# Two filter buffers outside the tables' room, a table in another's place, and the norms' transfer on the stores' queue

## The chip, the core and the metric

The kernel runs on one core of a Trainium2 chip. Its time is the device time of one execution in microseconds. One more execution was recorded by the profiler; the profile and all answers of its trace are of that one.

## What is computed

Four convolution blocks follow one another on an input of 32 images with 96 channels of 56 by 56 points. Each block normalises its input over groups of three channels and adds its result to the input:

```python
x = x + L0(_gn(x))   # 1x1 expand to 576, 3x3 depthwise, squeeze-excite, 1x1 project
x = x + L1(_gn(x))   # wavelet convolution, three Haar levels, 5x5 depthwise on each
x = x + L2(_gn(x))   # 1x1, 3x3 depthwise, 1x1 with weights and activations rounded to 4 bits
x = x + L3(_gn(x))   # 9x9 depthwise; its kernel is worked out from diff_metric

def _gn(v, G=32, eps=1e-5):
    g = v.reshape(B_, G, C_ // G, H_, W_)
    m = jnp.mean(g, axis=(2, 3, 4), keepdims=True)
    s = jnp.var(g, axis=(2, 3, 4), keepdims=True)
    return ((g - m) / jnp.sqrt(s + eps)).reshape(v.shape)
```

## The kernel before

**Layers 0 and 2 run image by image**, with channels on the partitions. Within them the order of PE, DVE and ACT is written out by hand, in the lists `L0_ORDER` and `L2_ORDER`: each entry is a step, a block of channels and a part of it (`e` expand, `f` first tap, `t` one of the other eight taps, `a` and `c` depthwise on PE, `p` project, `d` add, `o` store), and `+` and `-` shift it by an image. SP and POOL are not in these lists. A planner orders them from costs and due times of its own, and it also orders everything that stands outside such a list. The waits are put in by the framework.

**Layers 1 and 3 run channel by channel**, with image rows on the partitions. There a convolution is a product with a banded matrix for each channel, and SP's order is written out too. Layer 1 takes two channels (a pair) per turn and loads three turns ahead; layer 3 loads four channels ahead (`AHEAD`), and the norms of eight channels (`NN`) at once.

**Layer 0's taps.** Three blocks of an image are filtered on DVE. For each, ACT writes the first tap into one of five buffers `h2s` (L327), DVE adds the other eight taps (L332), and ACT ends the block (L338). Image b uses buffers 3b, 3b+1 and 3b+2, modulo five. In the order's list image 0 begins with `f0`, its later steps contain `f1 m+ t11`, and `f2 a0 t17 t21` come near the end. `m`, `q`, `v`, `w`, `b` and `n` are the steps of the next image's normalisation: negative mean (DVE, L282), sum of squares (ACT, L273), group sum (PE, L278), deviation (DVE L286, then a power on POOL, L288), bias (DVE L292), and the normalised image (ACT, L301).

**The tables.** `tables()` is called while layer 0 starts. `diffusion_kernels` works out layer 3's 9x9 kernels, on DVE and then on POOL. `wavelet_filters` spreads layer 1's filters into three padded tables `zt0`, `zt1`, `zt2` (cleared by POOL at L499, filled by DVE at L510), and SP stores them to DRAM (L511). `diffusion_filters` then clears the first half of `zt1` again (L1127), fills it on POOL (L1125, L1134), and SP stores it as `zdiff` (L1135). The tables lie in two pools which are closed before the pool `late` is opened in their room. Of the five tap buffers, one is allocated before the tables and four in `late`, next to `hab`, `wg` and `hc`:

```python
h2s = [cp.tile([128, H, W], F32, tag="h2", name="h2")]
tables()
late = ctx.enter_context(tc.tile_pool(name="l0l", bufs=1))
h2s += [late.tile([128, H, W], F32, tag=f"h2{i}", name=f"h2{i}") for i in range(3)]
h2s.append(late.tile([128, H, W], F32, tag="h23", name="h23"))
```

From the stored tables, SP copies the banded matrices of all channels from DRAM to DRAM during layer 0 (L522, L549), a few after each image.

**The hand-over between the layers.** The last image of layers 0 and 2 is stored by quarters as soon as each is added: four quarters by six groups of channels, 24 transfers (`store_tile`, L156). Then `store_norm` turns the means and variances of all images into one row per channel (factors, offsets, a bias) and sends it to DRAM from ACT's queue (L120). Layer 1 reads it back with `load_norm` (L600), layer 3 with `load_norms` (L1156), each broadcast to 128 partitions; both need it for their first operation on DVE (L671, L1169). In layer 1's list of loads the two channels' inputs X (L555, L558), matrices (L583 to L585, L656, L658) come first and both norms last; before the list stand four constants (L621). In layer 3 the norms come after the loads of four channels.

Of the kernel before, what the change touches and what calls it, by code (L numbers as in the profile page):

```python
# [10 lines left out]
F32 = mybir.dt.float32  # L11
# [4 lines left out]
ALU = mybir.AluOpType  # L16
# [4 lines left out]
B, C, H, W = 32, 96, 56, 56  # L21
# [59 lines left out]
            nc.sync.dma_start(t, w[n])  # L81


def power(nc, pool, out, in_, e, tag):

    ex = pool.tile(list(in_.shape), F32, tag=f"ex{tag}", name=f"ex{tag}")
    nc.gpsimd.memset(ex, e)
    nc.gpsimd.tensor_tensor(out, in_, ex, ALU.pow)


def channel_stats(nc, pool, x, mv, tag):

    st = pool.tile([C, 2 * NP, 6], F32, tag=f"st{tag}", name=f"st{tag}", bufs=2)
# [2 lines left out]
    nc.vector.bn_aggr(mv, st.rearrange("c a b -> c (a b)"))  # L96


def store_norm(nc, S, pool, psum, mv, dram, bias):


    mc, d, dv, ve = (pool.tile([C, B], F32, tag=f"n{n}", name=f"n{n}", bufs=1) for n in ("mc", "d", "dv", "ve"))
    row = pool.tile([C, 2 * B + 1], F32, tag="row", name="row", bufs=1)
    rstd = row[:, 0:B]
    ps = psum.tile([128, 2, 512], F32, tag="mm", name="pn")
    nc.vector.tensor_copy(mc, mv[:, :, 0])
    nc.tensor.matmul(ps[:C, 0, :B], S.grp, mc, start=True, stop=True)
    nc.vector.tensor_tensor(d, mc, ps[:C, 0, :B], ALU.subtract)
    nc.vector.tensor_tensor(dv, d, d, ALU.mult)
    nc.vector.tensor_tensor(dv, dv, mv[:, :, 1], ALU.add)  # L110
    nc.vector.tensor_tensor(d, mc, d, ALU.subtract)
    nc.tensor.matmul(ps[:C, 1, :B], S.grp, dv, start=True, stop=True)
    nc.vector.tensor_scalar(ve, ps[:C, 1, :B], EPS_GN, None, ALU.add)
    nc.gpsimd.tensor_tensor(rstd, ve, S.mhalf[:C, :B], ALU.pow)
    nc.vector.scalar_tensor_tensor(row[:, B : 2 * B], d, -1.0, rstd, ALU.mult, ALU.mult)
    if bias is None:
        nc.vector.memset(row[:, 2 * B :], 0.0)
    else:
        nc.vector.tensor_copy(row[:, 2 * B :], bias)
    nc.scalar.dma_start(dram, row)  # L120


def run_steps(step, image, order):
# [47 lines left out]
def layer0(ctx, tc, S, x, w, y0, norm1, tables, aside):  # L171
# [9 lines left out]
    nc = tc.nc  # L181
# [57 lines left out]
    diag = cp.tile([128, 2, 9, HALF], F32, tag="diag", name="diag")  # L239
    hpad = padded(cp, nc, 4, F32, "hpad")  # L240
    mv_all = cp.tile([C, B, 2], F32, tag="mv0", name="mv0")
    h2s = [cp.tile([128, H, W], F32, tag="h2", name="h2")]


    tables()
# [2 lines left out]
        for t in range(9):  # L248
            nc.vector.tensor_scalar(diag[:, k - AB, t, :], eye2, wdw[:, COL[k], t : t + 1], None, ALU.mult)
    late = ctx.enter_context(tc.tile_pool(name="l0l", bufs=1))  # L250
    h2s += [late.tile([128, H, W], F32, tag=f"h2{i}", name=f"h2{i}") for i in range(3)]
    hab = late.tile([128, NP, 2, NT], F32, tag="hab", name="hab")
    wg = late.tile([128, ND + 1, C], F32, tag="wg", name="wg")
    h2s.append(late.tile([128, H, W], F32, tag="h23", name="h23"))
    hc = late.tile([128, 2, 2, NT], F32, tag="hc", name="hc")

    ims = {}
# [188 lines left out]
    }  # L446
    with tc.manual_schedule(engines=MANUAL):
        run_steps(step, image, L0_ORDER)
    store_norm(nc, S, sm, psum, mv_all, norm1, S.bias1)


NK = 3
# [2 lines left out]
KW = 5  # L455


def wavelet_filters(nc, cp, cp2, w, z1, z2, z3):
# [14 lines left out]
    nc.vector.tensor_scalar(ws, ws, 0.25, None, ALU.mult)  # L473
    for v, z in enumerate((z1, z2, z3)):
# [12 lines left out]
        G = cp.tile([C, 3, 3, 25], F32, tag="G", name="G")  # L487
        for da in (-1, 0, 1):
            for dp in (-1, 0, 1):
                g = G[:, da + 1, dp + 1]  # L490
                nc.vector.tensor_copy(g, F[:, abs(da), abs(dp)])
                if v == 0:
                    gb = g.rearrange("c (e k) -> c e k", k=KW)[:, 1:4, 1:4]
                    nc.vector.tensor_tensor(gb, gb, base[:, 1 + da : 6 + da : 2, 1 - dp : 6 - dp : 2], ALU.add)
        groups = 2 if v < 2 else 1
        ks = NK if v < 2 else KW
        P = 2 * groups
        Z = (cp2 if v else cp).tile([C, 2, P, LEN, P, ks], F32, tag=f"z{v}", name=f"zt{v}")
        nc.gpsimd.memset(Z, 0.0)  # L499
        for ai in range(2):  # L500
            for ao in range(2):
                rows = slice(MIDL + ao - ai - 4, MIDL + ao - ai + 5, 2)
                for pi in range(P):
                    for po in range(P):

                        d = pi // 2 - po // 2
                        valid = [K for K in range(ks) if abs(groups * (K - ks // 2) + d) <= 2]
                        k0 = groups * (valid[0] - ks // 2) + d + 2
                        g = G[:, ao - ai + 1, po % 2 - pi % 2 + 1].rearrange("c (e k) -> c e k", k=KW)
                        nc.vector.tensor_copy(Z[:, ai, pi, rows, po, valid[0] : valid[-1] + 1], g[:, :, k0::groups])  # L510
        nc.sync.dma_start(z, Z.rearrange("c a p e o k -> c a p (e o k)"))  # L511
        if v == 1:
            room = Z[:, 0]
    return room


def toeplitz(nc, dst, z, phases, rows, step, first, row):
# [87 lines left out]
def layer1(ctx, tc, w, y0, norm, t1, t2, t3, y1, behind):  # L605
# [41 lines left out]
    def load(i):  # L647

        st = {"i": i, **sets[i % NF], "X": [], "T": [None] * 2, "nr": [], "raw": [], "raw2": []}
        for c in (2 * i, 2 * i + 1):  # L650
            X = io.tile([128, 2, B, W4], F32, tag="X", name="X", bufs=8)
            load_halves(nc, X, y0[c // GR][c % GR])
            st["X"].append(X)
            st["raw"].append(load_matrices(nc, pool, t1, c))
            raw = pool.tile([PH, NK * PH], F32, tag="raw2", name="raw2", bufs=4)
            nc.sync.dma_start(raw, t2[c])  # L656
            st["raw2"].append(raw)
            nc.sync.dma_start(st["T3"][c % 2 * HH : (c % 2 + 1) * HH, c % 2], t3[c])  # L658
        for c in (2 * i, 2 * i + 1):
            st["nr"].append(load_norm(nc, norms, norm, c))  # L660
        return st

    def normal(st, j, h):
# [219 lines left out]
def layer2(ctx, tc, S, k2, y1, y2, norm3):  # L883
# [203 lines left out]
    }  # L1087
    with tc.manual_schedule(engines=MANUAL):
        run_steps(step, image, L2_ORDER)
    store_norm(nc, S, sm, psum, mv_all, norm3, None)  # L1090


def diffusion_kernels(nc, cp, w):
# [9 lines left out]
        nc.vector.scalar_tensor_tensor(z[:, i, :], yy[:, 1, :], dm[:, 2 * i + 1 : 2 * i + 2], z[:, i, :],  # L1103
                                       ALU.mult, ALU.add)
    nc.vector.tensor_tensor(z, z, z, ALU.mult)
    r2, arg, two, kern, poi = (cp.tile([C, n], F32, tag=t, name=t) for t in ("r2", "arg", "two", "kern", "poi"))
    nc.vector.tensor_tensor(r2, z[:, 0], z[:, 1], ALU.add)
    nc.vector.tensor_scalar(arg, r2, K_EXP2, None, ALU.mult)
    nc.vector.tensor_scalar(r2, r2, TP * TP, None, ALU.add)

    nc.gpsimd.memset(two, 2.0)
    nc.gpsimd.tensor_tensor(kern, two, arg, ALU.pow)
    power(nc, cp, poi, r2, -1.5, "poi")
    nc.gpsimd.tensor_scalar(kern, kern, K_GAUSS, None, ALU.mult)
    nc.gpsimd.tensor_scalar(poi, poi, K_POI, None, ALU.mult)
    nc.gpsimd.tensor_tensor(kern, poi, kern, ALU.add)
    return kern


# [19 lines left out]
def layer3(ctx, tc, w, y2, norm, td, out):  # L1139
# [40 lines left out]
    with tc.manual_schedule(engines=MANUAL_SP):  # L1180
        for c in range(AHEAD):
            load(c)
        load_norms(0)
        for c in range(-2, C):
            if 0 <= c < C - AHEAD:
                load_norms(c + AHEAD)
# [15 lines left out]
def kernel_body(tc, w, x, out):  # L1202
    nc = tc.nc
    with ExitStack() as ctx:
# [22 lines left out]
        t3 = scratch("twav3", [C, HH, KW * HH])  # L1227

        def tables():
            with tc.tile_pool(name="tables", bufs=1) as tp, tc.tile_pool(name="tables2", bufs=1) as tp2:  # L1230
                kernels = diffusion_kernels(nc, tp2, w)
                room = wavelet_filters(nc, tp, tp2, w, z1, z2, z3)
                diffusion_filters(nc, tp2, kernels, zd, room)

        layer0(tc, S, x, w, y0, norm1, tables,
               [lambda c=c: wavelet_matrices(nc, z1, z2, z3, t1, t2, t3, c) for c in range(C)]
# [134 lines left out]
```

## Time and profile before

| | |
|---|---|
| median of 3 runs | 6552.63 us (6536.49 to 6554.98) |
| profiled execution, its own time | 6547.21 us |
| its span | 6545.4 us |
| PE busy | 6046.6 us (92%) |
| DVE busy | 5167.2 us (79%) |
| ACT busy | 3955.6 us (60%) |
| POOL busy | 223.0 us (3%) |
| DMA, mean | 69 GB/s, 452.93 MB |

The span is what the profiler saw of the execution; the time is measured around it. Rows headed PE, DVE and GB/s cut the span into 40 equal slices of 163.6 us, and each digit is the busy share in tenths. In lists of waits a line names the engine and line that waited, the releaser, the sum in us, how many times, and the longest. In timelines a row has the start and the length in us, the engine (SPq is SP issuing a transfer), the line, the operation, output and input with shapes, how many were merged, and in square brackets the idle time before and what ended it. The chain of waits gives start, length and what ran or was waited for.

### The profile page before, as it was taken

The page shows a single profiled execution, that of the slowest core. Times are in us where ns is not written, and L with a number is a line of the kernel's source. Part 1 is how long each engine was busy: PE and PEld are TensorE (multiplying, and loading weights), DVE is VectorE, ACT ScalarE, POOL GpSimd, SP SyncE. Part 2 cuts the span into 40 slices and gives each one's busy share as a digit, 9 for nine tenths or more (in the row PEclk, how much of TensorE's full clock was granted, in tenths as well). Part 3 has the DMA queues.
Part 4 walks back from the last instruction along what each step waited for, and adds up shares of the span by engine and source line. Part 5 has one row for each costly group of instructions (what it writes and reads, how often), then busy time and mean ns, then how long its engine had stood idle before and what let it go on. Part 6 is the DMA issues. An engine that isn't in the chain of part 4 may idle for free.

```text
span 6545.4 us, 115343 instructions
## 1 busy us (share of the span) xinstructions
PE 6046.6 (92%) x49064; PEld 3627.6 (55%) x49064; DVE 5167.2 (79%) x5468; ACT 3955.6 (60%) x5268; POOL 223.0 (3%) x158
## 2 busy tenths in 40 slices
PE   5989989998998998999969999989999999999699
PEld 3444444444444454445435556567777777778344
DVE  8989989898998998989947666657676767676577
ACT  5556556665666656565535555557676767677355
POOL 4000000000000000000000000000000000000000
PEclk8989989999999999999979999989999999999899
DMA  2375475639538459563755766655869585853788
GB/s 80 27 41 51 41 44 40 47 48 37 46 41 42 48 39 44 36 44 43 10 60 144 138 146 145 144 43 39 52 42 52 40 52 39 52 40 30 159 254 248
DMA packets 1631553, 452.93 MB, mean 69 GB/s; under 512 B 1447406, under 2 KB 1625318, under 8 KB 1627582
## 3 DMA queue, kind: packets, MB, share of 16 engines
q1 hardware_dynamic: 1630814, 445.50, 62.6%
q8 instruction: 386, 6.32, 0.6%
q14 instruction: 129, 1.06, 0.1%
q10 hardware_dynamic: 224, 0.05, 0.0%
HBM read 284.44 MB, written 214.08 MB: 76 GB/s over the span
## 4 chain that ended last, share of the span: by engine, by line
PE 71%; ACT 8%; DMA 6%; SPq 6%; DVE 4%; issue 3%; POOL 1%; POOLq 0%; ACTq 0%; DVEq 0%
PE psd L355 14%; PE psd L1022 10%; PE ps L315 9%; PE psj L413 8%; PE pc L1177 6%; PE ps L1003 6%; PE pc L738 5%; SPq L431 5%; DMA y<-xt 3%; PE psj L1059 3%; PE psj L415 2%; PE psj L416 2%; DVE h L332 2%; ACT hi L975 2%; ACT a L993 2%
## 5 line engine op out<-in xcount | busy, mean ns | idle before, releaser
L332 DVE SCALAR_TENSOR_TENSOR h<-hpad,l_wdw,h 128x3136 f32<-128x3136 f32 x768 | 2659.9, 3481 | 64.2 <-ACT h L327 35.9
L355 PE MATMUL psd<-hpad,diag 64*64 64x392 f32 x13824 | 1245.6, 513 | 31.2 <-issue 31.2
L319 ACT ACTIVATE hpad<-ps,o,s 128x784 f32<-128x784 f32 x640 | 685.0, 1081 | 778.3 <-PE ps L315 775.9
L315 PE MATMUL ps<-xn,l_wexp 96*128 96x392 f32 x2560 | 940.8, 520 | 107.2 <-ACT hpad L319 102.4
L1022 PE MATMUL psd<-apad,diag 64*64 64x392 bf16 x20736 | 929.8, 332 | 105.8 <-ACT a L993 51.6
L355 PEld LDWEIGHTS psd<-hpad,diag 64*64 64x64 f32 x13824 | 570.9, 132 | 694.8 <-issue 648.4
L1022 PEld LDWEIGHTS <-diag 64*64 64x64 bf16 x20736 | 692.2, 107 | 339.2 <-issue 159.1
L315 PEld LDWEIGHTS ps<-xn,l_wexp 96*128 96x128 f32 x2560 | 497.9, 199 | 500.9 <-ACT hpad L319 108.6
L567 ACT COPY T<-raw 32x112 f32<-32x112 f32 (+2 forms) x1440 | 462.6, 384 | 316.5 <-DMA raw<-tdiff 231.8
L993 ACT ACTIVATE u<-ps,o,s 128x784 int16<-128x784 f32 x576 | 536.9, 1003 | 161.1 <-PE ps L1003 142.8
L993 ACT ACTIVATE a<-psd,o,s 128x784 int16<-128x784 f32 x448 | 424.2, 999 | 320.9 <-PE psd L1022 320.9
L413 PE MATMUL psj<-h,wg 128*96 128x392 f32 x1536 | 591.5, 520 | 24.9 <-ACT hpad L319 23.4
L1003 PE MATMUL ps<-hi,l_w1q 96*128 96x392 f32 x1280 | 462.7, 362 | 9.3 <-ACT hi L975 9.2
L1177 PE MATMUL pc<-x,T 128*112 128x416 f32 (+1 forms) x1152 | 415.0, 523 | 58.0 <-DMA raw<-tdiff 58.0
L738 PE MATMUL pc<-x,T 128*112 128x416 f32 (+1 forms) x1152 | 451.2, 528 | 0.0
L1003 PE MATMUL ps<-lo,l_w1q 96*128 96x392 f32 x1280 | 438.3, 342 | 0.0
L413 PEld LDWEIGHTS psj<-h,wg 128*96 128x96 f32 x1536 | 249.1, 166 | 285.0 <-issue 257.4
L1177 PEld LDWEIGHTS pc<-x,T 128*112 128x112 f32 x1152 | 204.8, 178 | 267.7 <-issue 250.8
L338 ACT ACTIVATE hab<-psd,o,s 128x392 f32<-128x392 f32 x256 | 170.9, 672 | 291.2 <-PE psd L355 291.2
L338 ACT ACTIVATE h<-h,o,s 128x3136 f32<-128x3136 f32 x96 | 288.0, 3000 | 17.1 <-DVE h L332 17.1
L327 ACT ACTIVATE h<-hpad,l_wdw 128x3136 f32<-128x3136 f32 x96 | 279.1, 2908 | 31.4 <-DMA zdiff<-zt 30.4
L738 PEld LDWEIGHTS pc<-x,T 128*112 128x112 f32 x1152 | 192.7, 180 | 146.1 <-issue 146.1
(201 smaller groups left out, 6790.5 us busy)
## 6 DMA issues: line engine op xcount, KB each, us to landing
X<-y SPq DMA_DIRECT2D x192, 392.0 KB
xt<-in_x_dram SPq DMA_DIRECT2D x32, 1176.0 KB
y<-xt SPq DMA_DIRECT2D x192, 196.0 KB
y<-y SPq DMA_DIRECT2D x96, 392.0 KB
xt<-y SPq DMA_DIRECT2D x96, 392.0 KB
out_dram<-y SPq DMA_DIRECT2D x96, 392.0 KB
y<-xt SPq DMA_DIRECT2D x90, 392.0 KB
twav<-zwav SPq DMA_DIRECT2D x768, 36.8 KB
```

Source lines behind the costliest of these rows:

```text
L315: nc.tensor.matmul(ps[:, j, :NT], wexp[:, k * 128 : k * 128 + 128], im["xn"][:, j, rows, :].rearrange("c h w -> c (h w)"), start=True, sto ...
L319: nc.scalar.activation(window(im["pad"][k], 128, 0, 0, 2 * i * RT, 2 * RT).rearrange("p r (w j) -> p j r w", j=2), ps[:, :, :NT].rearrange ...
L332: nc.vector.scalar_tensor_tensor(h2, window(im["pad"][k], 128, t // 3 - 1, t % 3 - 1, 0, H), wdw[:, k, t : t + 1], h2, ALU.mult, ALU.add,)
L338: nc.scalar.activation(view, ps, AF.Silu, bias=bi[1][:, c : c + 1], scale=sc[1][:, c : c + 1], accum_out=accum)
L355: nc.tensor.matmul(ps[c * HALF : (c + 1) * HALF, j, :NT].rearrange("p (r w) -> p r w", w=W2), diag[p, k - AB, t, :], v[:, :, j:W:2], start ...
L413: nc.tensor.matmul(out.rearrange("c (r w) -> c r w", w=W2), wg[:, k, :], im["h2"][k][:, rows, j::2], start=(k == 0), stop=False)
L567: nc.scalar.copy(to.rearrange("x t (p s) -> x t p s", p=NPH), v[:, k])
L738: nc.tensor.matmul(ps[:PH, to], st["T"][j][:, h, k, :], st["x"][:, j, h, of], start=False, stop=(n == NK - 1))
L993: nc.scalar.activation(out, ps, AF.Identity, bias=o[:, c : c + 1], scale=s[:, c : c + 1])
L1003: nc.tensor.matmul(ps[:, j, :NT], w1[:, k * 128 : k * 128 + 128], im[part][:, r0 : r0 + RT, :].rearrange("c h w -> c (h w)"), start=(part ...
L1022: nc.tensor.matmul(ps[q, j, :NT].rearrange("p (r w) -> p r w", w=W), diag[p, k, t, :], v, start=(t == 0), stop=(t == 8))
L1177: nc.tensor.matmul(ps[:, :, to], st["T"][:, h, k, :], st["x"][:, h, :, of], start=(n == 0), stop=(n == NK - 1))
```

## The change

- Two of the five tap buffers are allocated before the tables; the other three stay in `late`.
- All tables share one pool. The third wavelet table takes the room of the first after that is stored, and is cleared by DVE instead of POOL. The diffusion kernels reuse their own inputs' room in place of five temporary tiles; the helper `power` is dissolved.
- `store_norm` sends its row from SP, pinned behind all that SP was given before it.
- In layer 1, each channel's norms are loaded right behind its X. In layer 3, the first eight channels' norms are loaded right behind channel 0 instead of behind channel 3.

```diff
-    nc.scalar.dma_start(dram, row)
+    tc.keep_in_program_order(nc.sync.dma_start(dram, row))
...
-    h2s = [cp.tile([128, H, W], F32, tag="h2", name="h2")]
+    h2s = [cp.tile([128, H, W], F32, tag=f"h2{i}", name=f"h2{i}") for i in range(2)]
...
-    h2s += [late.tile([128, H, W], F32, tag=f"h2{i}", name=f"h2{i}") for i in range(3)]
+    h2s += [late.tile([128, H, W], F32, tag=f"h2{i}", name=f"h2{i}") for i in (2, 3)]
...
-    h2s.append(late.tile([128, H, W], F32, tag="h23", name="h23"))
+    h2s.append(late.tile([128, H, W], F32, tag="h24", name="h24"))
...
-        Z = (cp2 if v else cp).tile([C, 2, P, LEN, P, ks], F32, tag=f"z{v}", name=f"zt{v}")
-        nc.gpsimd.memset(Z, 0.0)
+        if v < 2:
+            Z = rooms[v] = cp.tile([C, 2, P, LEN, P, ks], F32, tag=f"z{v}", name=f"zt{v}")
+        else:
+            n = 2 * P * LEN * P * ks
+            Z = rooms[0].rearrange("c a p e o k -> c (a p e o k)")[:, :n].rearrange(
+                "c (a p e o k) -> c a p e o k", a=2, p=P, e=LEN, o=P)
+        (nc.gpsimd if v < 2 else nc.vector).memset(Z, 0.0)
...
             load_halves(nc, X, y0[c // GR][c % GR])
             st["X"].append(X)
+            st["nr"].append(load_norm(nc, norms, norm, c))
             st["raw"].append(load_matrices(nc, pool, t1, c))
...
-        for c in (2 * i, 2 * i + 1):
-            st["nr"].append(load_norm(nc, norms, norm, c))
...
-    r2, arg, two, kern, poi = (cp.tile([C, n], F32, tag=t, name=t) for t in ("r2", "arg", "two", "kern", "poi"))
+    r2, arg, kern = z[:, 0], z[:, 1], yy[:, 0]
...
-    nc.gpsimd.memset(two, 2.0)
-    nc.gpsimd.tensor_tensor(kern, two, arg, ALU.pow)
-    power(nc, cp, poi, r2, -1.5, "poi")
+    nc.gpsimd.memset(yy[:, 0], 2.0)
+    nc.gpsimd.memset(yy[:, 1], -1.5)
+    nc.gpsimd.tensor_tensor(kern, yy[:, 0], arg, ALU.pow)
+    nc.gpsimd.tensor_tensor(r2, r2, yy[:, 1], ALU.pow)
...
         for c in range(AHEAD):
             load(c)
-        load_norms(0)
+            load_norms(c)
...
-            with tc.tile_pool(name="tables", bufs=1) as tp, tc.tile_pool(name="tables2", bufs=1) as tp2:
-                kernels = diffusion_kernels(nc, tp2, w)
-                room = wavelet_filters(nc, tp, tp2, w, z1, z2, z3)
-                diffusion_filters(nc, tp2, kernels, zd, room)
+            with tc.tile_pool(name="tables", bufs=1) as tp:
+                kernels = diffusion_kernels(nc, tp, w)
+                room = wavelet_filters(nc, tp, w, z1, z2, z3)
+                diffusion_filters(nc, tp, kernels, zd, room)
```

More of the change, by code (lines that the diff above doesn't have):

```diff
@@ L81, in load @@
             nc.sync.dma_start(t, w[n])
[L84 to L88, printed above, removed]
 def channel_stats(nc, pool, x, mv, tag):
@@ L96, in channel_stats, with store_norm @@
     nc.vector.bn_aggr(mv, st.rearrange("c a b -> c (a b)"))
-def store_norm(nc, S, pool, psum, mv, dram, bias):
+def store_norm(tc, S, pool, psum, mv, dram, bias):
+    nc = tc.nc
     mc, d, dv, ve = (pool.tile([C, B], F32, tag=f"n{n}", name=f"n{n}", bufs=1) for n in ("mc", "d", "dv", "ve"))
@@ L448, in layer0 @@
         run_steps(step, image, L0_ORDER)
-    store_norm(nc, S, sm, psum, mv_all, norm1, S.bias1)
+    store_norm(tc, S, sm, psum, mv_all, norm1, S.bias1)
 NK = 3
@@ L455, with wavelet_filters @@
 KW = 5
-def wavelet_filters(nc, cp, cp2, w, z1, z2, z3):
+def wavelet_filters(nc, cp, w, z1, z2, z3):
     wb = cp.tile([C, 50], F32, tag="wb", name="wb")
@@ L473, in wavelet_filters @@
     nc.vector.tensor_scalar(ws, ws, 0.25, None, ALU.mult)
+    rooms = {}
     for v, z in enumerate((z1, z2, z3)):
@@ L511, in wavelet_filters @@
         nc.sync.dma_start(z, Z.rearrange("c a p e o k -> c a p (e o k)"))
-        if v == 1:
-            room = Z[:, 0]
-    return room
+    return rooms[1][:, 0]
 def toeplitz(nc, dst, z, phases, rows, step, first, row):
@@ L1089, in layer2 @@
         run_steps(step, image, L2_ORDER)
-    store_norm(nc, S, sm, psum, mv_all, norm3, None)
+    store_norm(tc, S, sm, psum, mv_all, norm3, None)
 def diffusion_kernels(nc, cp, w):
@@ L1109, in diffusion_kernels @@
     nc.vector.tensor_scalar(r2, r2, TP * TP, None, ALU.add)
-    nc.gpsimd.memset(two, 2.0)
-    nc.gpsimd.tensor_tensor(kern, two, arg, ALU.pow)
-    power(nc, cp, poi, r2, -1.5, "poi")
+    nc.gpsimd.memset(yy[:, 0], 2.0)
+    nc.gpsimd.memset(yy[:, 1], -1.5)
+    nc.gpsimd.tensor_tensor(kern, yy[:, 0], arg, ALU.pow)
+    nc.gpsimd.tensor_tensor(r2, r2, yy[:, 1], ALU.pow)
     nc.gpsimd.tensor_scalar(kern, kern, K_GAUSS, None, ALU.mult)
-    nc.gpsimd.tensor_scalar(poi, poi, K_POI, None, ALU.mult)
-    nc.gpsimd.tensor_tensor(kern, poi, kern, ALU.add)
+    nc.gpsimd.tensor_scalar(r2, r2, K_POI, None, ALU.mult)
+    nc.gpsimd.tensor_tensor(kern, r2, kern, ALU.add)
     return kern
```

## The prediction

> **What bounds the kernel now.** I read the slices of the page first, then the list of waits, then the timelines of single engines around the three places that the diff touches.
>
> ```profile
> PE   5989989998998998999969999989999999999699
> DVE  8989989898998998989947666657676767676577
> GB/s 80 27 41 51 41 44 40 47 48 37 46 41 42 48 39 44 36 44 43 10 60 144 138 146 145 144 43 39 52 42 52 40 52 39 52 40 30 159 254 248
> ```
>
> PE is at 9 nearly everywhere, and DVE is close behind it in the first 20 slices (layer 0). Speed inside the stages is not for this diff: it changes nothing in the steady loops. What it can move are the three dips of PE: slice 1 (start), slice 20 (layer 0 to 1, where GB/s is 10) and slice 37 (layer 2 to 3).
>
> *Start.* ACT, DVE and POOL timelines:
>
> ```profile
> 79.09 2.91 ACT L327 ACTIVATE h<-hpad,l_wdw 128x3136 f32<-128x3136 f32 x1 [30.35 <-DMA zdiff<-zt]
> ```
> ```profile
> 67.43 0.15 DVE L282 TENSOR_SCALAR nm<-pn 96x1 f32<-96x1 f32 x1
> 82.03 6.88 DVE L332 SCALAR_TENSOR_TENSOR h<-hpad,l_wdw,h 128x3136 f32<-128x3136 f32 x2 [14.45 <-DMA twav<-zwav]
> ```
> ```profile
> 64.11 3.46 POOL L1125 COPY rev<-kern 96x9 f32<-96x9 f32 x1
> 67.88 0.19 POOL L1125 COPY rev<-kern 96x9 f32<-96x9 f32 x1
> 71.91 1.29 POOL L1134 COPY zt<-rev 96x18 f32<-96x18 f32 x8
> ```
>
> The first tap f1 goes into the second filter buffer, which lies in the pool opened where the tables closed; it waits for the last transfer of all tables. DVE then idles 14.45 us, and has no gap after it (busy 19.89 of the 20 us from 100 to 120, 29.79 of the 30 from 120 to 150). So its next start decides. The POOL rows matter later: the same copy takes 3.46 us while DVE runs taps and 0.19 us once DVE is idle.
>
> *Layer 0 to 1.* SP's waits in 3320 to 3380, chain, DVE timeline:
>
> ```profile
> SPq L156 <- DMA norm<-row: 9.3, 1, 9.3
> ```
> ```profile
> 3362.59 1.48 DMA norm<-row
> 3365.07 0.95 SPq L156
> 3366.06 1.03 SPq L156
> 3367.87 7.05 DMA y<-xt
> 3385.78 3.81 DMA nr<-norm
> ```
> ```profile
> 3389.66 0.92 DVE L671 TENSOR_TENSOR x<-X,nr 128x448 f32<-128x448 f32 x1 [8.63 <-DMA nr<-norm]
> ```
>
> A y store waits for the norms' transfer, with which it has nothing to do: the program has eight completion semaphores for transfers and gives them out in turn over both queues; norm<-row was ordered among the 24 last stores, and the 19th store takes the same semaphore. Six stores sit behind it.
>
> *Layer 2 to 3*, the same: the wait is 7.0 us long, and the norms come after four channels' loads.
>
> ```profile
> 6106.45 0.30 SPq L555 DMA_DIRECT2D X<-y  x1
> 6119.30 0.42 SPq L1156 DMA_DIRECT2D nr<-norm  x1
> ```
> ```profile
> 6124.19 0.62 DVE L1169 TENSOR_TENSOR x<-X,nr 128x448 f32<-128x448 f32 x1 [50.48 <-DMA X<-y]
> 6125.77 24.40 PE L1177 MATMUL pc<-x,T 128*112 128x448 f32 x61 [58.03 <-DMA raw<-tdiff]
> ```
>
> The reader should see that PE waits for x, x for nr, and nr for its place in SP's list.
>
> **The change part by part.**
>
> *1. Start.* Two buffers now lie before the tables, so f1 follows its expansions on ACT at 48.7 instead of 79.09, and q+ follows nm (67.43) at once. DVE could go on at 67.6: gain 14.4. Against it:
> - The third table is cleared on DVE (96x2520), which has no gap between 24 and 67. Nearest row: POOL's clear of this tile, 2.20 us. Bounds: 0.2 (a small DVE operation), and 2.8 (the 3.48 us tap scaled from 3136 to 2520 elements). I take 2.2. It also waits until the first table's store (2.3 MB, issued at 33.47) has read it: the DMA share is 0.97 from 35 to 45 and 0.64 from 45 to 50, so some 44 to 46; DVE reaches the third table's copies at 48.6. Free; if the planner places the clear right behind the second table (40.1), it costs up to 5 us, with the taps queued behind it. POOL's lost 2.20 us (13.3 to 15.4) was off the path.
> - The fewer temporaries: two small POOL memsets (0.16 us each) wait for DVE's last reading of the grid, at 24.8; the power starts at 25.78. 0.3 us, hidden.
> - POOL now copies the diffusion table beside running taps. With nm at 69.6, DVE runs t11 and t08 to 76.7 and t12 to t14 to 87.2. POOL passes two copies per tap (57.2 to 64.1: four in two taps). The nine rev copies end at 74.7 instead of 68.1; then the 2.61 us memset. Here a rule bears: the Trainium skill, "SBUF — State Buffer", "Who interferes with whom", says that a two-input DVE operation blocks GpSimd's reads, not its pure writes. No row here shows a memset under taps. By the rule it ends at 77.3, by the copies' rows (3.5 us) at 78.2. I take the rule; the sum differs by less than 1 us. Of 16 copies some five pass by 87.2; then DVE stands, because b+ needs rstd, which POOL holds behind them. The other 11 take 0.16 each: 89.0; rstd 0.57; t15 starts at 89.9 instead of 99.58. Gain **9.7**.
> - f2 still goes to a buffer over the tables: zdiff is issued at 89.1 and lands 5.8 later (73.23 to 79.05 before), 94.9; f2 ends at 97.8, and its tap t21 is due at 100.3. Slack 2.5 us, so nothing.
> Bounds of this part: 1.8 (rival 1) to 14.4.
>
> *2. norm<-row on SP behind the stores.* A rule of the skill speaks against any gain: "DMA: Bandwidth & Descriptors", "Issuing engines are not separate DMA queues": transfers of all issuing engines share the same 16 engines, so another queue saves issue time only. By it, moving 24 KB is worth 0, and costs one SP issue (0.35 us). By the rows, the wait of 9.3 and 7.0 us goes. The rule is about transfer, the row is about a wait at the issuer; I take the row.
> - Layer 0 to 1: six stores go on at 3354.8 instead of 3364.1. The DMA had emptied by 3357 before; now they queue (about 1.5 us each), so I take 8.4 of 9.3. Layer 1's first load then issues at 3366.7 instead of 3375.07. norm<-row is issued at about 3362.6 as before (its row is ready at 3362.56): its landing is beside the stores'.
> - Layer 2 to 3: 7.0 off. But the row's tile belongs to a pool that layer 3 reuses, and its transfer now comes last; alone it took 1.44 us. I take 1.0, so 6.0. First X load at 6100.4.
>
> *3. The norms' place in layer 1's list.* T0 is the first constant load. Before: nr issued at T0+10.3, x at T0+14.6. Now nr(0) follows X(0): T0+3.9. A raw load issued there (3378.94) had landed by 3382.44, 3.5 us; nr takes 3.8. So x starts at T0+7.7. The step's other loads move back 0.45 us each. Channel 1's x needs nr at T0+12.5, DVE is free at 12.8; ACT's matrix copies of channel 1 end at 16.4, xh at 17.3, xl at 18.4: lowest1 at T0+18.4 instead of 24.9 (3399.96). Gain 6.5. For the next pair nr no longer stands behind the raw load that waits for ACT (3.0 us); that keeps pace and is not counted.
>
> *4. In layer 3.* nr(0) follows load(0): T0+3.2 instead of 12.85. Its earlier landing took 4.9 us; x at T0+8.1 instead of 17.7; loads 1 to 3 move back by one issue and 266 KB, about 1.2 us. T(0) was ready at T0+7.4, PE then runs at its 4.3 us per channel (415.0/96), slower than loads (3.2 us issue). Gain 9.6.
>
> Sum: 9.7 + (8.4 + 6.5) + (6.0 + 9.6) = **40.2 us**. On the profiled execution 6547.2 - 40 = 6507; the median of the runs shown is 5.4 above it, so **6512**. Nothing gives it back: each place has only bound work behind it (DVE in layer 0, PE at 18.0 us per pair in layer 1, PE in layer 3). The eight waits for x in layer 0 (118.4 us) hang on stores that move with DVE.
>
> **The rivals.**
> 1. *The start is given back.* If the planner puts rstd before POOL's table copies, DVE never stands at b+, POOL crawls at two copies per tap, zdiff lands near 105, and t21 waits for f2 until 108.2 instead of 110.0. Gain 1.8, time 6520. Against it: before, the copies came first. Chance 0.2.
> 2. *Hidden anyway.* The last stores are limited by the DMA and not by the issue: busy share 9 from 6080 to 6102 speaks for it, the empty 6070 to 6075 against. Then part 2 gives about 3 instead of 14.4, and the loads crowd the norms: parts 3 and 4 give half (8). With the start at 9.7: 6532. Chance 0.1. If the planner still orders norm<-row among the stores, part 2 is 0: the same case.
> 3. *Slower.* SP's list in layer 0 is ordered by the planner, which now sees an earlier start and a later third table. If its 192 filling jobs fall before x fetches, more images wait; the eight that do now lose 118.4/8 = 15 us each. From three more images on (44) the gain of 40 is used up; four cost 59, and the time is 6552.6 - 40 + 59 = 6572. Against it: the lists hang on the image's own stores. Chance 0.04.
> 4. *More.* POOL is not blocked under taps: start 14, time 6507. Chance 0.05.
>
> **How the numbers follow.** Main case 0.61, by itself 6500 to 6524 (part 1 from 5 to 12, the hand-overs each by 3, the runs' scatter by 8). A measurement here tells 0.3% (19.7 us, 6533) from no change. Faster: 0.61 + 0.2 + 0.05 and half of rival 2, rounded 0.91; same 0.06; slower 0.03. Range 6488 to 6533: it reaches over rivals 1, 4 and most of 2.
>
> **What would show it.** ACT L327's wait for zdiff gone at 48.7; POOL's L1134 copies at up to 3.5 us; DVE's idle before t15 2 to 3 us, with rstd as releaser; no "SPq L156 <- DMA norm<-row"; first L621 load about 8 us sooner after the last add; x (L671) 7.7 us after it; in layer 3 x 8 us after the first X load, and PE 10 us earlier against it. Wrong if: DVE stands at t21 (rival 1), the stores' own spacing grows by what the wait was (rival 2), or the list of waits has more than eight L273 waits for x (rival 3).

## The result, and the profile after

The kernel after takes 6498.39 us (median of 4 runs, 6495.52 to 6506.39) against 6546.09 us (median of 4 runs, 6536.49 to 6554.98): the ratio is 0.9929, 95% interval [0.991, 0.9949], 48 us less by the medians. The profiled executions are 46.05 us apart (6547.21 and 6501.16), and it is these that are taken apart here. The forecast of 6512 was 40 us less. So the total came out near; its terms, as the traces show, did not all.

The slices of the page of after, to be laid beside those of before:

```profile
PE   6989989998998998989969999989999999999699
DVE  8989979898998998989957766657777767676587
GB/s 80 29 41 50 41 43 41 46 44 40 47 41 41 43 47 42 39 41 39 17 60 143 141 155 150 143 36 45 48 42 50 44 49 41 51 38 31 166 253 248
```

The three dips are still there, and at 162 us a slice nothing finer can be read. The milestones of the two traces say more. "Last add" is the very last addition of a layer's last image on DVE; a low-band product is PE's first multiplication of a pair of channels in layer 1 (lowest1).

| stretch | before, us | after, us | gained |
|---|---|---|---|
| start to last add of layer 0 | 3349.7 | 3340.4 | 9.3 |
| to layer 1's first load | 25.3 | 21.3 | 4.0 |
| to the first low-band product | 23.8 | 17.2 | 6.6 |
| first to last low-band product (47 steps) | 878.4 | 855.6 | **22.8** |
| to layer 2's first product | 56.3 | 56.6 | -0.3 |
| to the last add of layer 2 | 1727.4 | 1733.5 | -6.1 |
| to layer 3's first load | 45.6 | 45.3 | **0.3** |
| to layer 3's first product | 19.3 | 9.2 | 10.2 |
| to the end | 419.7 | 420.3 | -0.7 |

*Start.* ACT's and DVE's timelines of after (start, duration, engine, line, what; in brackets the idle time before it and what ended that):

```profile
46.36 2.91 ACT L321 ACTIVATE h<-hpad,l_wdw 128x3136 f32<-128x3136 f32 x1
96.02 2.92 ACT L321 ACTIVATE h<-hpad,l_wdw 128x3136 f32<-128x3136 f32 x1 [8.26 <-DMA twav<-zwav]
```
```profile
49.00 2.16 DVE L499 MEMSET zt<- 96x2520 f32 x1 [0.47 <-issue]
...
71.23 0.15 DVE L276 TENSOR_SCALAR nm<-pn 96x1 f32<-96x1 f32 x1
...
90.86 0.16 DVE L286 TENSOR_TENSOR nb<-nm,rstd 96x1 f32<-96x1 f32 x1 [2.19 <-POOL rstd L282]
...
91.13 41.83 DVE L326 SCALAR_TENSOR_TENSOR h<-hpad,l_wdw,h 128x3136 f32<-128x3136 f32 x12
```

In before, the row that the last of these answers to:

```profile
99.58 48.75 DVE L332 SCALAR_TENSOR_TENSOR h<-hpad,l_wdw,h 128x3136 f32<-128x3136 f32 x14
```

POOL in after:

```profile
57.05 17.77 POOL L1123 COPY rev<-yy 96x9 f32<-96x9 f32 x9
74.76 2.61 POOL L1125 MEMSET zt<- 96x3024 f32 x1
77.44 12.85 POOL L1132 COPY zt<-rev 96x27 f32<-96x27 f32 x16
90.26 0.57 POOL L282 TENSOR_TENSOR rstd<-ve,mhalf 96x1 f32<-96x1 f32 x1
```

f1 runs at 46.36 with no wait, DVE stands 2.19 us for rstd as foreseen, and goes on at 91.13 instead of 99.58. f2 still waits for the tables (8.26 us on ACT), but no tap waits for f2: DVE's next row runs through 12 taps.

*Layer 0 to 1.* SP's first load of layer 1 in before, then SP's timeline and DVE's first norm operation of layer 1 in after:

```profile
3375.07 0.36 SPq L621 DMA_DIRECT2D low<-in_low_dram  x1
```
```profile
3331.64 23.19 SPq L150 DMA_DIRECT2D y<-xt  x14
3354.92 1.62 SPq L114 DMA_DIRECT2D norm<-row  x1
3361.70 0.36 SPq L619 DMA_DIRECT2D low<-in_low_dram  x1
```
```profile
3369.69 0.92 DVE L668 TENSOR_TENSOR x<-X,nr 128x448 f32<-128x448 f32 x1 [1.95 <-DMA nr<-norm]
```

The wait for norm<-row is gone and x comes 8.0 us after the first load, as forecast; but that load is only 4.0 us sooner after the last add, not 8.4.

*Layer 2 to 3.* SP's, DVE's and PE's timelines of after:

```profile
6020.17 42.51 SPq L150 DMA_DIRECT2D y<-xt  x24
6062.78 1.60 SPq L114 DMA_DIRECT2D norm<-row  x1
6069.83 0.31 SPq L553 DMA_DIRECT2D X<-y  x1
...
6073.01 0.42 SPq L1154 DMA_DIRECT2D nr<-norm  x1
```
```profile
6077.49 0.62 DVE L1167 TENSOR_TENSOR x<-X,nr 128x448 f32<-128x448 f32 x1 [40.16 <-DMA X<-y]
```
```profile
6078.99 6.47 PE L1175 MATMUL pc<-x,T 128*112 128x448 f32 x11 [47.61 <-DMA raw<-tdiff]
```

The norms come behind the first channel, x 7.7 us after the first load, PE 9.2 us after it. But the 24 stores take 42.5 us with no foreign wait among them, as long as the 42.1 us that they took in before with a wait of 7.0 us inside. SP's rows of before, all 24 stores and then the 18 behind the wait:

```profile
6056.54 42.08 SPq L156 DMA_DIRECT2D y<-xt  x24
```
```profile
6075.24 23.38 SPq L156 DMA_DIRECT2D y<-xt  x18
```

So the wait cost nothing here, but it did not simply run beside transfers. Five us of before inside the wait (stretch, its length, busy us of PE, PEld, DVE, ACT, POOL; clock, DMA share, GB/s) show the DMA almost still:

```profile
6070.00:6075.00 5.00, 0.00 (x0) 0.00 (x0) 0.19 (x1) 0.00 (x0) 3.48 (x1) 0.50 0.10 6
```

What took the wait back is the pace of the stores: the 18 behind it went at 1.30 us each, the 24 of after at 1.77 us.

*Inside layer 1.* This the forecast did not have. The list of waits of before and then of after, both from 3400 to 4260 (engine, line, waited for: total us, times, longest):

```profile
DVE x L671 <- DMA nr<-norm: 44.7, 7, 8.8
```
```profile
DVE x L668 <- DMA nr<-norm: 9.6, 4, 3.2
```

In before, DVE stood for nr five times for 7.4 to 8.8 us. Two of them in DVE's timeline, and SP's timeline ahead of the first:

```profile
3669.74 0.93 DVE L671 TENSOR_TENSOR x<-X,nr 128x448 f32<-128x448 f32 x1 [8.77 <-DMA nr<-norm]
...
3764.78 0.94 DVE L671 TENSOR_TENSOR x<-X,nr 128x448 f32<-128x448 f32 x1 [8.69 <-DMA nr<-norm]
```
```profile
3643.37 4.84 SPq L878 DMA_DIRECT2D xt<-y  x2
3648.26 7.04 SPq L555 DMA_DIRECT2D X<-y  x1
...
3666.79 0.83 SPq L600 DMA_DIRECT2D nr<-norm  x2
```

Two loads of layer 2's first images (xt<-y, k2.begin) and the load behind them hold SP for 11.9 us. The list of the next pair slips by that much, its norms stand last in it, and x waits for them. This happens once per channel group, five times in the layer; each time a pair takes some 22 to 23 us instead of 18.03, or two pairs share the loss. In after the two loads hold SP as long (11.5 to 12.5 us, 11.4 to 12.1 in before), but each nr stands right behind its image, ahead of the matrices that wait for ACT, and every step from the ninth on takes 18.0 us.

### The profile page after: what moved, and what is told of

Its sections match the earlier page's. It is cut to its first block, busy times and chain, and to the rows that moved or that the text cites. A ratio compares the mean times of both kernels' runs of the same rounds, so it can differ in the third digit from the quotient of the medians.

```text
span 6499.3 us, 115397 instructions
## 1 busy us (share of the span) xinstructions
PE 6025.5 (93%) x49064; PEld 3599.1 (55%) x49064; DVE 5168.3 (80%) x5469; ACT 3953.6 (61%) x5268; POOL 234.1 (4%) x157
## 4 chain that ended last, share of the span: by engine, by line
PE 71%; ACT 9%; DMA 9%; SPq 6%; DVE 3%; issue 1%; POOL 1%; ACTq 0%; DVEq 0%
PE psd L349 14%; PE psd L1019 11%; PE ps L309 9%; PE psj L407 8%; PE pc L735 6%; PE ps L1000 5%; SPq L425 4%; DMA y<-xt 4%; PE pc L1175 3%; PE psj L1056 3%; PE psj L409 3%; PE psj L410 2%; ACT hi L972 2%; ACT a L990 2%; DVE h L326 2%; PE pc L719 2%
## 5 line engine op out<-in xcount | busy, mean ns | idle before, releaser
L349 PEld LDWEIGHTS psd<-hpad,diag 64*64 64x64 f32 x13824 | 547.5, 132 | 694.9 <-issue 656.8
L407 PE MATMUL psj<-h,wg 128*96 128x392 f32 x1536 | 591.4, 520 | 27.9 <-ACT hpad L313 26.4
```

The costliest lines, as they stand in the source:

```text
L349: nc.tensor.matmul(ps[c * HALF : (c + 1) * HALF, j, :NT].rearrange("p (r w) -> p r w", w=W2), diag[p, k - AB, t, :], v[:, :, j:W:2], start ...
L407: nc.tensor.matmul(out.rearrange("c (r w) -> c r w", w=W2), wg[:, k, :], im["h2"][k][:, rows, j::2], start=(k == 0), stop=False)
```

## The experiments

The kernel before takes 6444 to 6460 us in these runs, on three chips, and 6546 us in the first comparison, whose chip is not named. That matters for part 2. "Us less" is worked out from the ratio to the runs of before beside it, unless medians are named; with gains this small the two can differ by some us.

**Each part alone on the kernel before.** Four kernels, on one chip, beside the same runs of before (6447.0 us).

*Part 1 alone*, the edit of tables, third table and filter buffers:

```diff
-    h2s = [cp.tile([128, H, W], F32, tag="h2", name="h2")]
+    h2s = [cp.tile([128, H, W], F32, tag=f"h2{i}", name=f"h2{i}") for i in range(2)]
...
+        (nc.gpsimd if v < 2 else nc.vector).memset(Z, 0.0)
```

> The kernel before with part 1 alone (two filter buffers ahead of the tables, the third table in the first one's room and cleared on DVE, fewer temporaries). Theory: DVE's next start moves from 99.6 to about 91.1 us as in the kernel after, 8.5 us, and nothing gives it back: last add of layer 0 near 3340, time 8 to 9.5 us less. Rival A (the start is given back in layer 0, where images wait for x): less than 4 us. Rival B (a part of the unforeseen gain in layer 1 comes from here): more than 14 us, and fewer waits of DVE for nr in layer 1.

Measured: 6441.24 us, ratio 0.9987 [0.9977, 0.9996], 8.4 us less. In the trace, the last add of layer 0 comes at 3235.3; in the six runs here that lack part 1 it comes at 3248.7 to 3252.8, in the six that have it at 3235.3 to 3245.4: 10.5 us by the means. Layer 1 is as uneven as in before. The interval of the times, 2.6 to 14.8 us, leaves room for both rivals' numbers; the traces do not. The theory holds.

*Part 2 alone:*

```diff
-    nc.scalar.dma_start(dram, row)
+    tc.keep_in_program_order(nc.sync.dma_start(dram, row))
```

> The kernel before with part 2 alone (norm<-row issued on SP behind the last stores). Theory read from the two traces: the last 24 stores of each layer are limited by the transfers, so that the wait for norm<-row mostly hid behind them; the first load of layer 1 comes 4 us sooner after the last add (21.8 instead of 25.9), that of layer 3 0.3 us sooner: 3 to 5 us less in all. Rival (the prediction's own step): 8.4 + 6.0 = 14.4 us less.

Measured: 6436.66 us, ratio 0.9979 [0.997, 0.9988], 13.5 us less. That is the rival's number, and the theory read from the first pair of traces falls on this chip. The first load of layer 1 comes 17.2 us after the last add instead of 24.3 to 24.7, that of layer 3 33.2 us instead of 41.3 to 41.8. SP's timeline and its list of waits at the second hand-over with norm<-row on ACT (the kernel with part 1 alone), and then its timeline with norm<-row on SP:

```profile
5931.00 40.06 SPq L150 DMA_DIRECT2D y<-xt  x24
```
```profile
SPq L150 <- DMA norm<-row: 14.2, 1, 14.2
```
```profile
5954.03 30.43 SPq L157 DMA_DIRECT2D y<-xt  x24
5984.56 1.85 SPq L121 DMA_DIRECT2D norm<-row  x1
5991.60 0.31 SPq L556 DMA_DIRECT2D X<-y  x1
```

Without a wait the same 24 stores take 30.4 us here, and 42.5 us in the first comparison. Here the wait is 14.2 us long, since SP reaches it sooner, and 9.6 us of it lengthen the list; there it was 7.0 us and lengthened nothing. So the question became whether the wait's worth hangs on what is queued in front of it; the last pair of experiments asks that.

*Part 3 alone:*

```diff
+            st["nr"].append(load_norm(nc, norms, norm, c))
             st["raw"].append(load_matrices(nc, pool, t1, c))
...
-        for c in (2 * i, 2 * i + 1):
-            st["nr"].append(load_norm(nc, norms, norm, c))
```

> The kernel before with part 3 alone (each channel's norms loaded right behind its image in layer 1). Theory: 6.5 us at the start of layer 1 as predicted, and 22.8 us more inside the layer, where DVE waited five times 7.4 to 8.8 us for nr and each time PE lost about 4.6 us: 27 to 31 us less, layer 1 in even steps of 18.0 us per pair. Rival A (the prediction: nothing inside the layer): 6.5 us less. Rival B (the five long pairs went for another reason, such as the moved start of the layer): 6.5 us less, and pairs of 22 us remain.

Measured: 6420.74 us, ratio 0.9951 [0.9933, 0.997], 31.6 us less. The first low-band product comes 16.9 us after the first load instead of 23.4 to 24.0, and from the first to the last it takes 855.4 us instead of 881.7 to 882.7 in the three others. The theory holds, both rivals fall.

*Part 4 alone:*

```diff
             load(c)
-        load_norms(0)
+            load_norms(c)
```

> The kernel before with part 4 alone (norms of the first eight channels behind channel 0's loads in layer 3). Theory and prediction agree: x 8 us after the first load instead of 17.7, PE 10 us sooner against it, 9 to 10.5 us less. Rival (the loads behind it are late instead, and the gain is given back inside layer 3): less than 5 us, with gaps on PE in the first ten channels.

Measured: 6442.8 us, ratio 0.999 [0.9978, 1.0002]: 6.4 us less, which by itself can't be told from nothing. The trace can: PE's first product comes 9.8 us after the first load instead of 18.0 to 19.1, and layer 3 takes 420.9 us from there, as in the others (419.5 to 420.2). The gain is there and is not given back in layer 3; in the time it is smaller than the scatter of layer 2 (below).

**All parts together, again.**

> The kernel after, unchanged, on the chip of the other experiments, on which the kernel before takes 6447 us and the last stores of a layer run faster. Theory (the parts add up, and each is worth what it was worth alone there: 8 for the start, 13 for the norms' queue, 32 for layer 1, 7 to 10 for layer 3): 52 to 66 us less than before. Rival (parts share one wait, and what one gains another can't): 40 to 48 us less, as in the first comparison.

Measured on another chip than the parts, beside before at 6452.03 us: 6390.61 us, ratio 0.9902 [0.9888, 0.9917], 63 us less. The four parts alone sum to 60 by their ratios (47 by the medians, where the whole is 61). By their stretches in the traces they sum to 70: 10.5 for the start, 7.9 + 9.2 for the norms' queue, 7.1 + 26.4 for layer 1, 9.3 for layer 3. The parts add up; the rival falls. The change is worth more here than in the first comparison because part 2 is.

**Part 2 undone in the kernel after.**

```diff
-    tc.keep_in_program_order(nc.sync.dma_start(dram, row))
+    nc.scalar.dma_start(dram, row)
```

> The kernel after with part 2 alone undone (norm<-row issued on ACT again, not pinned). Theory (the stores of this chip run faster than those of the first comparison, so that less of the wait hides behind them): a wait of SP for norm<-row of 12 to 14 us comes back at both hand-overs, the first load of layer 1 comes 24 us after the last add instead of 17 and that of layer 3 41.5 us instead of 33; 12 to 16 us slower than the kernel after. Rival (the wait is hidden by the stores whatever the chip): the waits come back and the time is within 5 us of the kernel after.

Measured: 6401.27 us, ratio to before 0.9923 [0.9909, 0.9936]: 10.7 us slower than the kernel after by the medians, 13.5 by the ratios. The wait of 14.2 us comes back, the first load of layer 1 is at 24.1 us after the last add (16.9 in the kernel after), that of layer 3 at 41.6 (31.4). The theory holds.

**What makes nr late in layer 1.** In the kernel before, layer 1's loop no longer calls k2.begin itself:

```diff
             k2.prepare(pair)
-            if not k2.stages:
-                k2.begin(min(2 * pair, C - GR))
```

> The kernel before, in which layer 1 issues none of layer 2's first image loads (xt<-y, two pairs of images, one channel group at a time); all of them come at its end. Theory (the five waits of DVE for nr in layer 1 come where SP's list is held up by these loads, which wait for the group's stores, and nr is last in the list): the five waits of 8 us go, although the norms' place is unchanged, the steps of layer 1 are 18.0 us throughout, and layer 1 takes 855 to 860 us from its first to its last low-band product instead of 882; at the hand-over to layer 2 the loads, 2.4 MB, then stand open, and 20 to 50 us are lost. Rival (nr is late because its place behind the second raw load waits for ACT's matrix copies, whatever else is in the list): five or more waits of 7 us or more remain and layer 1 takes 875 us or more.

The edit did not do quite what was said: outside the order written out by hand, the planner put the loads back among layer 1's, but one by one, the two of a group two to three pairs of channels apart. So no late loads were tried. Measured: 6420.51 us, ratio 0.9949 [0.9932, 0.9966], 32.9 us less than before with the norms where they were. The waits of DVE from 3300 to 4175:

```profile
DVE x L671 <- DMA nr<-norm: 9.5, 6, 3.1
```

No wait of 7 us or more is left and layer 1 takes 855.5 us from its first to its last low-band product. The rival falls: the norms' place alone did not make the stall. It took both, the place at the end of the list and two of these loads back to back; either cure brings the whole of it. By SP's rows, a load that stands apart is issued in 0.6 us. Of two together the second takes 3.9 to 4.8 us to issue and the load of X behind it 6.5 to 7.0 us, so that the list is some 11 to 12 us later.

**What hides the wait for norm<-row.** A backlog was put in front of the last stores, in a kernel with norm<-row on ACT and in one with it on SP:

```diff
             for to, of in groups(im["xt"], y2, lambda y: y[:, :, b, :], store=True):
                 nc.sync.dma_start(to, of)
+            for to, of in list(groups(im["xt"], y1, lambda y: y[:, :, b, :], store=True))[:3]:
+                nc.sync.dma_start(to, of)
```

> The kernel before, with three more stores of the last image but one in layer 2 (groups 0 to 2, 196 KB each in pieces of 56 bytes, to a part of y1 that is no longer read), ahead of the last image's 24 stores: a backlog of some 16 to 20 us, such as slower stores would leave. Read beside backlog_norm_on_sp, by the first load of layer 3 after the last add (41.5 us without the backlog). Theory (the wait for norm<-row runs beside the draining of what is queued): the wait shrinks from 15 us to 0 to 5, the first load comes at 45 to 52. Rival (the wait costs its length whatever is queued): the wait stays at 12 us or more, the first load comes at 57 or later.

> The same backlog with part 2 (norm<-row on SP behind the last stores). Theory: the first load of layer 3 comes within 2 us of that of backlog_before, where it came 8.2 us sooner without a backlog; at the hand-over from layer 0, where there is no backlog, part 2 is still worth 7 us between the last add and the first constant's load. Rival: 8 us sooner than in backlog_before here too.

SP's list of waits and its timeline with norm<-row on ACT, then the timeline with it on SP:

```profile
SPq L156 <- DMA norm<-row: 7.3, 1, 7.3
```
```profile
5945.81 16.39 SPq L1078 DMA_DIRECT2D y<-xt  x3
5962.29 40.53 SPq L156 DMA_DIRECT2D y<-xt  x24
6008.59 0.30 SPq L555 DMA_DIRECT2D X<-y  x1
```
```profile
5946.46 15.96 SPq L1079 DMA_DIRECT2D y<-xt  x3
5962.52 40.29 SPq L157 DMA_DIRECT2D y<-xt  x24
6002.91 0.85 SPq L121 DMA_DIRECT2D norm<-row  x1
6008.21 0.31 SPq L556 DMA_DIRECT2D X<-y  x1
```

Each of the two ran once, and only their traces are read. The wait shrinks to 7.3 us, more than the 0 to 5 expected, and it costs nothing: the first load of layer 3 comes 51.4 us after the last add with the wait and 51.9 without it. At the hand-over from layer 0, which has no backlog, part 2 still cuts the way to the first load from 24.2 to 16.0 us. So a queue ahead of the wait takes its cost away. The theory's reason is not what the rows show. With norm<-row on ACT the DMA nearly stops here too (2 GB/s or less from 5974 to 5978), and the 21 stores behind the wait then go faster:

```profile
5977.36 25.45 SPq L156 DMA_DIRECT2D y<-xt  x21
```

That is 1.21 us each, where the 24 of the kernel with norm<-row on SP take 1.68 us each. Why stores behind a pause go faster is open.

The first comparison had such a queue of its own. From the first of the 24 stores on, the DMA moved more pieces of 56 bytes than the 21504 of the stores themselves: 2210 more in before and 2587 in after, 3935 to 4011 with the added backlog, and 0 to 77 in seven of the other traces (counted in the traces' packets). That its stores are slower as such is not shown: behind the wait they ran at 1.30 us there, and at 1.27 us in the kernel with part 2 alone.

**A version built on this.** If the last stores' drain sets layer 3's start, its first load should not stand behind all of them. In the kernel after, the last image's stores of groups 0 and 1 were put ahead of norm<-row and the other 16 into layer 3's list:

```diff
+            nc.sync.dma_start(*parts[0])
+            for g in range(1, C // GR):
+                rest[g].append(parts[g])
...
+    for part in rest[1]:
+        tc.keep_in_program_order(nc.sync.dma_start(*part))
     store_norm(tc, S, sm, psum, mv_all, norm3, None)
...
                 load(c + AHEAD)
+            if rest and c % 2 == 0:
+                nc.sync.dma_start(*rest.pop(0))
```

> The kernel after, with the last image's 24 stores in layer 2 in another order: those of the first two channel groups ahead of the norms, the other 16 in layer 3's list, one behind every second channel's loads, so that layer 3's first load waits for the first group alone. Theory (the last stores are limited by their transfers, and layer 3's first load stands behind all of them): first load of layer 3 about 15 us after the last add (the norms' row is ready at 13.4) instead of 33 to 46, PE 9 us after it, layer 3 unchanged at 420 us: 17 to 30 us less than the kernel after. Rival A (the deferred stores, in pieces of 56 bytes, crowd the loads of layer 3, whose transfers take 0.87 of the time): layer 3 longer by 10 us or more and PE with gaps in its first 30 channels, less than 10 us gained. Rival B (norm<-row lands late behind the stores that are queued): x 15 us or more after the first load.

Measured: 6387.17 us, ratio to before 0.9906 [0.989, 0.9923], which is the kernel after's own. The first load comes 14.4 us after the last add instead of 31.4, and layer 3 then takes 438.6 us instead of 419.8: rival A, 17.0 us gained and 18.7 given back. Stretches of layer 3 in the kernel after and in this one (stretch, its length, busy us and number of instructions of PE, PEld, DVE, ACT, POOL; clock, DMA share, GB/s):

```profile
6055.00:6075.00 20.00, 20.00 (x57) 9.93 (x56) 16.76 (x29) 10.50 (x32) 0.00 (x0) 1.00 0.90 263
```
```profile
6010.00:6030.00 20.00, 17.48 (x48) 7.88 (x47) 13.91 (x24) 9.60 (x28) 0.00 (x0) 1.00 0.84 234
6050.00:6070.00 20.00, 17.09 (x47) 7.87 (x46) 13.81 (x24) 9.58 (x28) 0.00 (x0) 1.00 0.80 230
```

PE does 47 or 48 products in 20 us where it did 57; the two stretches are among those that lose most. Two more spacings were tried, `c > 0 and c % 4 == 2` in place of `c % 2 == 0`, and the same with AHEAD 5:

> The kernel after with the last image's stores split as in the run before (first two channel groups ahead of the norms, 16 stores in layer 3's list), but one store behind every fourth channel's loads, from channel 2 on, instead of every second. Theory (layer 3's transfers take 0.87 of the time, so some 0.13 of 4.37 us, 0.57 us, is free per channel; a store took about 1.4 us of the transfers, which four channels can hold and two can't): layer 3 421 to 426 us instead of 438.6, first load 14.4 us after the last add, 10 to 17 us less than the kernel after. Rival (every deferred store costs PE its own time wherever it is put, 18.7/16 = 1.2 us each): layer 3 438 us again, same time as the kernel after within 5 us.

> As the run beside it, and layer 3's loads run five channels ahead instead of four. Theory (the lead holds what a store delays): layer 3 at 420 to 422 us, 0 to 4 us better than with four ahead. Rival (the lead isn't what is short; one more 266 KB load crowds the start): PE's first product in layer 3 no sooner, and the same time or up to 3 us more.

Measured: 6375.5 us, ratio 0.9889 [0.9872, 0.9906], and 6384.35 us, ratio 0.9908 [0.9891, 0.9924], beside before at 6443.94. Neither can be told from the kernel after. Layer 3 took 444.2 and 439.9 us in the profiled executions: the rival's case, a deferred store costs PE 1.2 to 1.3 us wherever it is put (18.7/16, 20.0/16). The 444.2 would make it 1.5 us, but that execution took 6400.85 us where the four others of its kernel took 6374.87 to 6379.17, and does not stand for them. The theory's free 0.57 us per channel could not be used. Why is open: while PE stands the DMA share is no higher than in the kernel after (0.80 and 0.84 in the stretches shown, 0.81 to 0.90 there), so the share gives no sign of running out; that the loads stand in line behind a store's 56-byte pieces is possible, but no run tells it apart.

## Why the prediction was right, and where it was not

The time and the sign were right, and the three places named were the right places. Step by step:

1. *Start*, 9.7 forecast, 8.45 measured at tap `t15`, 9.3 at the last add. The clear of the third table cost 2.16 us (2.2 forecast), the wait for rstd 2.19 (2.5). POOL's memset took 2.61 us beside running taps and the same in before, where DVE stood idle, as the rule of the Trainium skill ("SBUF — State Buffer", "Who interferes with whom") would have it, and ended at 77.4, where the rule gave 77.3; the nine copies ahead of it took 17.77 us, where one alone takes 0.19. Two small things were missing: the grid's load landed 1.0 us later in this execution, and DVE had two pauses of 0.5 us. The slack at f2 was enough. That 9.3 us were left at the last add of this pair is partly luck: from the eighth image to the thirtieth the lead was 2.4 to 5.1 us. It rose to 9.4 in the image after that, in which PE of before stood 4.0 us with no releaser on show:

```profile
3191.57 2.23 PE L355 MATMUL psd<-hpad,diag 64*64 64x392 f32 x11 [4.04 <-issue]
```

Such pauses of over 2.5 us come four times in layer 0 of this before (28.4 us), three times in this after (13.1 us) and in none of the twelve other traces; their cause is open. In those, six with part 1 and six without, the lead is 8.0 to 10.9 us by the means at every image: part 1 is worth about its forecast.

2. *norm<-row on SP*, 14.4 forecast, 4.3 in the first comparison, 17 in the other runs. This is one of two terms that were mis-sized. The step "six stores go on at 3354.8 instead of 3364.1 ... I take 8.4 of 9.3", and its twin of 6.0, took the gap in the list for time on the path, although the text of rival 2 named the evidence against it (DMA busy share 9 from 6080 to 6102). Rival 2's sign came true in this part, at the hand-over to layer 3 (stores at 1.77 instead of 1.30 us), and in this part only: parts 3 and 4 did not halve. The rule of the Trainium skill weighed there ("DMA: Bandwidth & Descriptors", "Issuing engines are not separate DMA queues") gave 0; the rows gave 14.4. The runs show that each comes near for one state of the queue: with a backlog of 16 us the move is worth -0.5 us, without it 8 to 9 us per hand-over.
3. *The norms' place in layer 1*, 6.5 forecast at the layer's start, 6.6 measured. (The forecast's T0+24.9 is PE's second product; the first stood at T0+23.8, and at T0+17.2 in after.) But "for the next pair nr no longer stands behind the raw load that waits for ACT (3.0 us); that keeps pace and is not counted" failed: it was worth 22.8 us more, over three times the term that was counted. The list of waits of before over its whole span has it, as its fortieth line: x waits for nr 53.4 us in all, eight times, of which only the first 8.6 were read. A wait that comes back every eighth pair is not seen in any timeline of a hand-over.
4. *Layer 3*, 9.6 forecast, 10.2 measured (9.3 in the other runs).

The sum was saved by chance: 10 us too much in part 2, 23 too little in part 3, and 6.1 us that layer 2 took longer in this execution. Layer 2's code is the same in all; between the same two milestones it took 1714 to 1743 us in the twelve experiments and 1727 and 1734 in the two first traces. That scatter of 29 us is as large as part 3's gain and two to three times that of any other part, and is why parts of 6 to 8 us show in stretches of a trace and hardly in a median. The kernels with all four parts lie in its upper half (1728 to 1743); whether that is more than chance is open.

Rival 1 (start given back) fell: the copies still come ahead of rstd. Rival 3 fell by its own sign: ACT's waits for x in layer 0 are eight as before. But they are 145 us long instead of 118, 27 us more where the start gained 8.45. Most of that is one wait, 25.5 us at 2827 instead of 6.8, and just ahead of it PE of before had paused for 13.0 us: at these places the image sets the pace, and time won or lost ahead of it goes into the wait. So did the lead: at the wait near 880, which grew from 23.6 to 27.0 us, it fell from 6.5 to 3.0 us. In the prediction's first view PE's dip between layers 0 and 1 and the 10 GB/s are not in one slice: the 10 GB/s stand in the slice before the dip.

## What to carry to other kernels

Read the list of waits by line over the whole span before reading timelines of the places that a change seems to be about: a wait of 8 us that comes back five times is worth more than the gap at the hand-over that draws the eye. What a wait in an issuing queue costs depends on what is queued in front of it: of 14.2 us, 9.6 counted where little was queued, and of 7.0 us none where the queue was still long. So look at what was queued in front, and expect the same edit to be worth more or less in another run of the same kernel. In a list that is worked in order, put what is small and wanted first ahead of what may wait, so that a hold-up anywhere before it does not reach the engine.

## What was not expected of the hardware

The same kernel differs between the first comparison and the other runs by more than the change is worth: before takes 6546 us in the one and 6444 to 6460 in the others. Much of it lies in layer 0, whose last add comes at 3349.7 in the first and at 3248.7 to 3252.8 in the others without part 1; ACT's waits for x there are 112.1 us (from 60 us on) against 53.8 to 59.9, and PE's pauses without a releaser are 28.4 us against none. Whether it is the chip is not shown.

The 24 stores of 49 KB in pieces of 56 bytes take 29.7 to 30.4 us with little queued in front, 40.3 us behind a backlog of 16 us, and 42.5 us in the first comparison, all without a foreign wait.

A load in pieces of 112 bytes (xt<-y, 3584 pieces) was issued in 0.6 us when it stood alone, but two of them in a row held the list for over 11 us, most of it (6.5 to 7.0 us) in the issue of the load of X that came next. Who pays is what stands behind them, which has nothing to do with them.
